# Two conditional MLP layers on one core: a third group of four, another order of units, and the sort of the second layer's choices off VectorE

## The chip, the cores and the metric

The kernel runs on one core of a Trainium2 chip, all in float32. The metric is the device time of one execution in microseconds (us); the number compared is the median of the runs. Engines are named as in the profile: PE (TensorE), DVE (VectorE), ACT (ScalarE), POOL (GpSimd), SP (SyncE, which here issues most DMAs); PEld is PE's weight load.

## The reference

There are 16 batches of 256 rows by 256 features, and 8 numbers for each batch that choose experts. Two layers are added to the input one after the other.

```python
# layer one: one expert of 8 for each batch
expert = jnp.argmax(opcode_onehot, axis=-1)
up   = x @ W_up[expert].T + b_up[expert]        # 256 -> 512
gate = x @ W_gate[expert].T + b_gate[expert]
x = x + (silu(up) * gate) @ W_down[expert].T + b_down[expert]

# layer two: the two best experts of 8, weighted, and one shared expert
w, sel = top_k(softmax(router_logits), 2);  w = w / w.sum()
mlp(x, g, u, d) = (gelu(x @ g) * (x @ u)) @ d   # 256 -> 1024 -> 256
x = x + sum_k w[k] * mlp(x, expert sel[k]) + mlp(x, shared)
```

So layer one has 16 pieces of work (a batch with its expert), layer two has 32 chosen pieces and 16 that all use the shared expert.

## The kernel before

**Units.** Pieces that use the same expert are put together. A `Pair` takes two pieces of one expert and multiplies the two batches by the weights with a seven-product scheme in place of eight (`STEPS`): seven products for each quarter of the hidden width, on sums of weight blocks (`sums_q`, `sums_d`, made by POOL) and sums of the inputs (`sums_b`, on DVE). A first-layer pair has 2 quarters, a second-layer pair 4. A product is two matmuls of 128x128 by 128x256, and the profile has two PE passes for each float32 matmul. ACT copies a bank (L637), DVE combines copies and banks (L645), ACT applies silu or gelu, DVE multiplies by the other half (L708) and makes the sums for the down product. The seven down products of a pair (`down`, L746) are not run at its end: `line.later` puts them between the up products (L660) of the unit that follows, from `first` on and `step` apart. A `Single` does one piece by plain products. A `Quad` takes four batches of the shared expert with 26 products (`BLOCK`) for each of two halves of the hidden width, in place of 28 for two pairs; its weight factors are made once by `prepare`, which POOL and ACT run between the second-layer pairs, and wait in DRAM. `SEEDS`, `SUMS_AT`, `DOWNS_AT`, `ACT_AT` and `ACT_SUMS_AT` say after which product of a group a bank is seeded, sums are made, the downs of the group before run, and activations follow. The banks of PSUM are given out by `bank` in the order they come free.

**Order.** Each engine runs its instructions in the order written. `Line` writes it: `main` advances a clock with each product, `later` queues work for a clock time, `quarter` is called at each quarter and issues loads for the fifth quarter ahead and POOL's sums for the third ahead. The shared expert's first `2 * NF` batches are done by pairs (`shared`), the other by groups of four: `NF = 4` gives four pairs and two groups. The order of units is

1. two first-layer singles, then the first-layer pairs that are certain (four, `l0_pairs`);
2. a branch on a number made on the device (`arms(0)`): how many further pairs layer one has (`l0_more`). The profile's counts show three for this input. In this arm the shared pairs and the further first-layer pairs take turns: shared, further, shared, further, and so on;
3. the second-layer pairs (`pairs`), a second branch (`arms(1)`; three more pairs here), two second-layer singles and the groups of four.

`announces` says at which quarters each engine gets a hint of the arm to come, so that its code can be fetched.

**The choices.** To find what can be paired, the pieces are ordered by expert with comparisons of all with all. For layer one this runs at the start on 128 partitions (16x16 comparisons, same on each partition). For layer two `choices` computes the second-best experts and weights and `order_of_work` sorts the 32 pieces: comparisons of 32x32, so 1024 elements on each of 128 partitions, in twelve large steps and more small ones on DVE. These steps are not run at once: a `Recorder` (L251) stores each as a step, `routes` says how many are run at a quarter, and `route` runs them (so they stand in the profile under one line, L1459). All must be done before the second-layer pairs begin.

Of the kernel before, what the change touches and what calls it, by code (L numbers as in the profile page):

```python
# [8 lines left out]
F32 = mybir.dt.float32  # L9
I32 = mybir.dt.int32  # L10
AF = mybir.ActivationFunctionType
ALU = mybir.AluOpType
# [3 lines left out]
B, S, D, E = 16, 256, 256, 8  # L16
H0, H1 = 512, 1024
P = 128
# [3 lines left out]
NA = 2 * B  # L22
# [1 line left out]
NP1 = (B - 1 - E + 1) // 2  # L24
NP2 = (NA - E) // 2
NS1, NS2 = B - 1 - 2 * NP1, NA - 2 * NP2
NF = 4
N2 = 2 * S
QW = 2 * 4 * P
QB = QW + 4  # L30
# [29 lines left out]


RATIOS = (-1, 0, 1, 2)
BLOCK = ('P0', 'P1', 'P2', 'Q0', 'P3', 'W01', 'Q1', 'Q2', 'W02', 'N01', 'N10', 'Q3', 'W23', 'N02', 'N20', 'W12', 'N32', 'N23', 'W13', 'W03', 'N21', 'N13', 'N12', 'N03', 'N31', 'N30')
SEEDS = {'P1': ('01',), 'P2': ('02',), 'W02': ('23',), 'Q3': ('12',), 'W12': ('03',), 'N10': ('13',)}
SUMS_AT = ((4, (0, 2)), (4, (1, 2)), (10, (2, 3)), (22, (1, 3)), (30, (0, 3)))
DOWNS = (0, 2, 4, 1, 5, 3, 6)
DOWNS_AT = (8, 11, 12, 15, 19, 25, 27, 27, 33, 39, 46, 48, 49, 50)
ACT_AT, ACT_SUMS_AT = 10, 6
QUADS = (B - 2 * NF) // 4
FACTORS = 4  # L70
CHUNKS = 2 * len(BLOCK) // FACTORS
# [3 lines left out]
def kernel(  # L75
# [10 lines left out]
    nc = tc.nc  # L86
    SP, POOL, PE, DVE, ACT = (
        getattr(mybir.EngineType, e) for e in ("SP", "Pool", "PE", "DVE", "Activation")
    )
    ctx.enter_context(tc.manual_schedule())  # L90

    const = ctx.enter_context(tc.tile_pool(name="const", bufs=1))
# [10 lines left out]
    areas = {}  # L103
# [97 lines left out]
    def bank(of, seeded=False, half=False):  # L201
        ok = [i for i in psum["idle"] if psum["filled"][i] or not seeded]
        if psum["halves"]:
            ok = [i for i in ok if (i in psum["halves"]) == half]
            if not seeded and not half:
                ok.sort(key=lambda i: psum["filled"][i])
        assert ok, (of, seeded, psum, open_banks)
        i = ok[0]
        psum["idle"].remove(i)
        assert of not in open_banks  # L210
        open_banks[of] = i
        psum["filled"][i] = not half
        return banks[i]

    def done_with(of):
        psum["idle"].append(open_banks.pop(of))
# [22 lines left out]
    num = const.tile([P, NA], F32, name="num")  # L239
# [6 lines left out]
    ats = const.tile([P, NA], F32, name="ats")  # L246

    made = {}
    steps = [[]]

    class Recorder:  # L251


        def __getattr__(self, name):
            return lambda *args: steps[-1].append(partial(getattr(nc.vector, name), *args))

        @staticmethod
        def step():
            steps.append([])
# [5 lines left out]
    def as_index(v, dst, src, shift, most):  # L265
        v.tensor_scalar(dst, src, float(shift), float(most), ALU.add, ALU.min)
# [113 lines left out]
            v.tensor_scalar(nwsort, wsort, -1.0, None, ALU.mult)  # L380


    exs = [const.tile([P, n], I32, name=f"exs_{i}") for i, n in enumerate((B, NA))]
    bs = [const.tile([P, n], I32, name=f"bs_{i}") for i, n in enumerate((B, NA))]
    wsort = const.tile([P, NA], F32, name="wsort")
    nwsort = const.tile([P, NA], F32, name="nwsort")
    wts = const.tile([P, 2, B], F32, name="wts")
    more = const.tile([P, 1], F32, name="more")
    MOST = ((NS1 - 1) // 2, NS2 // 2)
    more_i = [const.tile([P, 1], I32, name=f"more_{i}") for i in range(2)]  # L390
# [3 lines left out]
    def choices(v):  # L394

        tt, red = v.tensor_tensor, v.tensor_reduce
        hot = [const.tile([P, B, E], F32, name=f"hot_{k}") for k in range(2)]
        tt(hot[0], em8b, over_experts(at1), ALU.is_equal)
        step(v)
        lg2 = const.tile([P, B, E], F32, name="lg2")  # L400
        v.tensor_scalar(lg2, hot[0], -2.0, 1.0, ALU.mult, ALU.add)
        step(v)
        v.scalar_tensor_tensor(lg2, lg2, FLT_MAX, lg, ALU.mult, ALU.min)
        step(v)
        first_largest(v, lg2, 2, at2)
        step(v)
        tt(hot[1], em8b, over_experts(at2), ALU.is_equal)
        step(v)
        v.tensor_scalar(ats, ats, float(-E), -1.0, ALU.max, ALU.min)
        tot = const.tile([P, B], F32, name="tot")  # L410
        red(tot, rw, AX.X, ALU.add)
        step(v)
        v.reciprocal(tot, tot)
        tt(rw, rw, over_experts(tot), ALU.mult)
        step(v)
        for k in range(2):
            tt(hot[k], rw, hot[k], ALU.mult)
            step(v)
            red(wts[:, k, :], hot[k], AX.X, ALU.add)
            step(v)  # L420
        den = const.tile([P, B], F32, name="den")
        tt(den, wts[:, 0, :], wts[:, 1, :], ALU.add)
        v.reciprocal(den, den)
        step(v)
        wsc = const.tile([P, 2, B], F32, name="wsc")
        for k in range(2):
            tt(wts[:, k, :], wts[:, k, :], den, ALU.mult)
        v.tensor_scalar(wsc, wts, SCALE, None, ALU.mult)
        v.scalar_tensor_tensor(wts, wts, 1.0 - SCALE, wsc, ALU.mult, ALU.add)
        step(v)  # L430
        order_of_work(v, NA, ats, 1)


    at_num = const.tile([P, 2, B], F32, name="at_num")
# [24 lines left out]
    class Unit:  # L459
# [4 lines left out]
        def __init__(self, n, layer, at, batches_at=None):  # L464
            self.n, self.layer, self.at, self.batches_at = n, layer, at, batches_at
            self.kp = KPS[layer]
            self.q, self.s, self.x_from = {}, {}, None

            self.d_from = "d" if layer or self.width == 2 else "s" if at < B - 2 else "xt"
            self.acts = []  # L470
# [99 lines left out]
    class Pair(Unit):  # L570
        width, last = 2, False
        behind = quad = None
        crowded = False
        first, step, apart_banks = 18, None, False
# [281 lines left out]
    class Quad(Unit):  # L856
# [4 lines left out]
        width, last, alone = 4, False, False  # L861
# [232 lines left out]
    class Single(Unit):  # L1094
        width = 1
# [177 lines left out]
    l0_pairs = [Pair(next(names), 0, 2 * i) for i in range(NP1)]  # L1273
    l0_more = [Pair(next(names), 0, 2 * NP1 + 2 * i) for i in range(MOST[0])]
    l0_ones = [Single(next(names), 0, 2 * NP1 + i) for i in range(NS1 - 1)]
    shared = [Pair(next(names), 1, None, (2 * i, 2 * i + 1)) for i in range(NF)]
    quads = [Quad(next(names), None, range(i, i + 4)) for i in range(2 * NF, B, 4)]
    first_quad = quads[0]
    first_quad.x_at = None
    pairs = [Pair(next(names), 1, 2 * i) for i in range(NP2)]  # L1280
# [5 lines left out]
    l0_pairs[0].behind = 1  # L1286
    for u in l0_pairs[:-1]:
        u.first = 16.5
    units = [l0_pairs, pairs[:-1]]
    tails = [shared[:1], pairs[-1:]]  # L1290


    announces = [
        [(l0_pairs[0], 0, [SP, POOL, ACT, DVE]), (l0_pairs[2], 1, [PE])],
        [
            (pairs[-7], 0, [SP]),
            (pairs[-5], 0, [POOL, ACT]),
# [5 lines left out]
    among = {  # L1303
        u: [[] for _ in range(u.kp)]
        for u in [*l0_pairs, *l0_more, *pairs, *more_pairs, *shared, *quads]
    }
# [25 lines left out]
    class Line:  # L1332
# [115 lines left out]
        def routes(self, unit, j):  # L1448


            if not unit.layer:
                return {2: 5, 3: 1, 5: 1, 6: 1}.get(self.at, 0)
            return 2 if unit is shared[1] and j < 3 else int(unit is not shared[0] or j > 0)

        def route(self):

# [25 lines left out]
    nc.vector.tensor_scalar(sort1, at1, float(-E), -1.0, ALU.max, ALU.min)  # L1482
    nc.vector.memset(sort1[:, 0:1], 0.0)
    order_of_work(nc.vector, B, sort1, 0, [partial(l0_first.up, j) for j in range(2)])
    choices(Recorder())
    steps.append([partial(give, "ys", "sq")])
    l0_one.load_q(0)
    l0_one.load_x()
# [43 lines left out]
    run(units[0])  # L1532
    for k in arms(0):

        mid, further = [], l0_more[:k]
        for i, u in enumerate(shared[:NF]):
            mid.append(u)
            if i < len(further):
                mid.append(further[i])
                u.step = 4  # L1540
        places = [a for u in mid for a in among[u]]
        for a in places:
            a.clear()
        pieces = [p for u in l0_ones[2 * k :] for p in (u.ups, u.downs)]
        for a, p in zip(places[4:], pieces):
            a.append(p)
        follow([*mid, *units[1], *tails[1]], behind=False)
        run([*mid, *units[1]])
        while line.routed < len(steps):
            line.route()  # L1550
        for k in arms(1):
            assert not line.preparing
            left = ones[2 * k :]
            rest = [*tails[1], *more_pairs[:k], *left[:-1], *quads, *left[-1:]]
            quads[-1].alone = not left
            last_pair = [*tails[1], *more_pairs[:k]][-1]
            last_pair.first, last_pair.step, last_pair.apart_banks = 14, 3, True
            for u in left[-1:]:
                u.x_from = "at"
            turns["xs"], turns["d"] = [0, 1], [*turns["d"], 2]  # L1560
            for u in rest:
                among[u] = [[] for _ in range(u.kp)]
            follow(rest)
            run(rest)
            line.flush(1 << 30)
            line.send()
# [58 lines left out]
```

## Time and profile before

| | |
|---|---|
| median of 3 runs | 1035.84 us (1035.65 to 1036.08) |
| profiled execution | 1034.93 us, of which span 1033.3 us |
| granted PE clock | 0.999 |
| PE | 1025.3 us busy, 4714 passes |
| DVE | 786.9 us busy |
| POOL | 494.3 us busy |
| ACT | 384.0 us busy |
| DMA | 156.97 MB, mean 152 GB/s |
| first-layer pairs in a row | about 24 to 91 us |
| shared and further first-layer pairs in turns | about 91 to 290 us |
| groups of four | from 868 us |

Busy time of PE is from the start of the first to the end of the last of overlapping passes, so a short stop between two passes hardly shows in it; the distance between starts shows it. The windows of the profile count passes, which shows the same.

### The profile page before, as it was taken

The page shows a single profiled execution, that of the slowest core. Times are in us where ns is not written, and L with a number is a line of the kernel's source. Part 1 is how long each engine was busy: PE and PEld are TensorE (multiplying, and loading weights), DVE is VectorE, ACT ScalarE, POOL GpSimd, SP SyncE. Part 2 cuts the span into 40 slices and gives each one's busy share as a digit, 9 for nine tenths or more (in the row PEclk, how much of TensorE's full clock was granted, in tenths as well). Part 3 has the DMA queues.
Part 4 walks back from the last instruction along what each step waited for, and adds up shares of the span by engine and source line. Part 5 has one row for each costly group of instructions (what it writes and reads, how often), then busy time and mean ns, then how long its engine had stood idle before and what let it go on. Part 6 is the DMA issues. An engine that isn't in the chain of part 4 may idle for free.

```text
span 1033.3 us, 14372 instructions
## 1 busy us (share of the span) xinstructions
PE 1025.3 (99%) x4714; PEld 894.5 (87%) x4714; DVE 786.9 (76%) x1250; ACT 384.0 (37%) x613; POOL 494.3 (48%) x553
## 2 busy tenths in 40 slices
PE   9999999999999999999999999999999999999998
PEld 7888888888888888888888888888888888888887
DVE  8899988878687878878777777778777643997661
ACT  2444353535333324333333333333333323653410
POOL 3965341312464889799567557638754301000001
PEclk9999999999999999999999999999999999999999
DMA  7655647466554576566335534514543455553423
GB/s 262 231 184 193 229 166 229 164 194 214 163 184 132 148 189 170 176 175 173 86 98 143 129 94 125 142 58 129 143 122 110 106 170 130 199 183 95 113 49 76
DMA packets 70528, 156.97 MB, mean 152 GB/s; under 512 B 8226, under 2 KB 38818, under 8 KB 66978
## 3 DMA queue, kind: packets, MB, share of 16 engines
q1 hardware_dynamic: 57170, 140.38, 41.0%
q0 software_dynamic: 12976, 15.21, 10.4%
q8 instruction: 43, 0.70, 0.3%
q14 instruction: 51, 0.42, 0.1%
q10 hardware_dynamic: 288, 0.26, 0.1%
HBM read 124.89 MB, written 30.93 MB: 151 GB/s over the span
## 4 chain that ended last, share of the span: by engine, by line
PE 93%; DVE 3%; POOL 2%; issue 1%; ACT 0%; DMA 0%; SPq 0%; POOLq 0%; DVEq 0%; ACTq 0%
PE bank L660 48%; PE bank L746 30%; PE bank L1030 9%; PE bank L1103 4%; PE bank L1136 2%; DVE c L645 1%; DVE bt L708 1%; PE bank L231 1%; POOL s L595 0%; DMA bt<-x_dram 0%; POOL s L597 0%; POOL s L598 0%; DVE bt L588 0%; POOL s L596 0%; ACT c L702 0%
## 5 line engine op out<-in xcount | busy, mean ns | idle before, releaser
L637 ACT ACTIVATE cp<-bank 128x512 f32<-128x512 f32 x270 | 160.9, 596 | 417.4 <-PE bank L660 416.9
L660 PE MATMUL bank<-xt,s 128*128 128x256 f32 x1216 | 288.6, 380 | 1.2 <-DVE c L645 1.2
L660 PEld LDWEIGHTS bank<-xt,s 128*128 128x128 f32 x1216 | 230.1, 190 | 35.4 <-DVE c L645 1.6
L645 DVE TENSOR_TENSOR c<-cp,bank 128x512 f32<-128x512 f32 x360 | 233.9, 679 | 35.1 <-ACT cp L637 17.7
L660 PE MATMUL bank<-xt,q 128*128 128x256 f32 x912 | 219.7, 379 | 0.0
L746 PE MATMUL bank<-bt,ds 128*128 128x256 f32 x816 | 195.7, 379 | 0.3 <-DVE dz L763 0.3
L660 PEld LDWEIGHTS bank<-xt,q 128*128 128x128 f32 x912 | 173.3, 190 | 23.6
L708 DVE TENSOR_TENSOR bt<-c 128x1024 f32<-128x1024 f32 x90 | 129.2, 1436 | 77.6 <-ACT c L702 75.6
L746 PEld LDWEIGHTS bank<-bt,ds 128*128 128x128 f32 x816 | 154.9, 190 | 22.0 <-POOL s L598 0.7
L557 POOL DMA_DIRECT2D out_dram<-ys x46 | 49.6, 1169 | 240.0 <-DVE ys L779 118.7
L746 PE MATMUL bank<-bt,d 128*128 128x256 f32 x572 | 137.0, 379 | 0.0
L746 PEld LDWEIGHTS bank<-bt,d 128*128 128x128 f32 x572 | 108.7, 190 | 14.8
L595 POOL TENSOR_TENSOR s<-q 128x256 f32<-128x256 f32 x78 | 77.8, 998 | 82.7 <-PE bank L660 49.7
L598 POOL TENSOR_TENSOR s<-s,q 128x256 f32<-128x256 f32 x78 | 66.2, 849 | 98.0 <-PE bank L660 91.3
L702 ACT ACTIVATE c<-c 128x1024 f32<-128x1024 f32 x76 | 79.9, 1051 | 9.7 <-DVE c L645 9.7
L588 DVE TENSOR_TENSOR bt<-bt 128x512 f32<-128x512 f32 x105 | 81.9, 780 | 0.5 <-DMA bt<-x_dram 0.5
L596 POOL TENSOR_TENSOR s<-s,q 128x256 f32<-128x256 f32 x78 | 77.5, 994 | 6.1
L597 POOL TENSOR_TENSOR s<-q 128x256 f32<-128x256 f32 x78 | 74.1, 950 | 0.2 <-PE bank L660 0.2
L590 DVE TENSOR_TENSOR bt<-bt 128x256 f32<-128x256 f32 x98 | 62.0, 633 | 3.4
L595 POOL TENSOR_TENSOR ds<-d 128x512 f32<-128x512 f32 (+1 forms) x21 | 24.7, 1178 | 79.1 <-DMA d<-wd_dram 51.0
L589 DVE TENSOR_TENSOR bt<-bt 128x256 f32<-128x256 f32 x98 | 59.3, 605 | 3.4
L1030 PE MATMUL bank<-xt,q 128*128 128x256 f32 x224 | 50.8, 379 | 0.0
(211 smaller groups left out, 1028.4 us busy)
## 6 DMA issues: line engine op xcount, KB each, us to landing
q<-wq_dram SPq DMA_DIRECT2D x98, 512.0 KB, 4.0
d<-wd_dram SPq DMA_DIRECT2D x19, 1024.0 KB, 5.8
q<-factors SPq DMA_DIRECT2D x26, 512.0 KB, 3.2
xt<-x1d SPq DMA_DIRECT2D x46, 256.0 KB, 5.0
out_dram<-ys POOLq DMA_DIRECT2D x46, 256.0 KB, 5.2
s<-qsums SPq DMA_DIRECT2D x12, 512.0 KB, 5.8
ds<-dsums SPq DMA_DIRECT2D x4, 1024.0 KB, 7.4
d<-wd_dram SPq DMA_DIRECT2D x7, 513.0 KB, 6.5
```

What stands on the lines that cost most here:

```text
L588: tt(more[:, 0:2, :], t[:, 0:3:2, :], t[:, 2:4, :], ALU.subtract)
L595: tt(s("S1"), a("A21"), a("A22"), ALU.add)
L596: tt(s("S2"), s("S1"), a("A11"), ALU.subtract)
L597: tt(s("nS3"), a("A21"), a("A11"), ALU.subtract)
L598: tt(s("nS4"), s("S2"), a("A12"), ALU.subtract)
L637: nc.scalar.activation(t, self.banks["X", j], AF.Copy)
L645: nc.vector.tensor_tensor(self.c[j][:, block].rearrange("p m s -> p (m s)"), self.copies[n, j], self.banks[tag, j], op,)
L660: nc.tensor.matmul(self.banks[tag, j][:, bass.ts(m, S)], lhsT=self.q[j][:, m, A_AT[a], :] if a in A_AT else self.s[j][:, m, S_AT[a], :], r ...
L702: nc.scalar.activation(u, u, AF.Gelu_apprx_tanh)
L708: nc.vector.tensor_tensor(t[:, 0:4, :], u, v, ALU.mult)
L746: nc.tensor.matmul(d, lhsT=src[:, j, :], rhs=self.act_block(j, b), start=OPENS[k] and j == 0, stop=j == self.kp - 1, skip_group_check=True,)
L1030: nc.tensor.matmul(dst[:, bass.ts(m, S)], lhsT=w[:, m, :], rhs=rhs, start=fresh and m == 0, stop=True, skip_group_check=True,)
```

## The change

`NF` goes from 4 to 2: two shared pairs and three groups of four. The order of products in a group, its seeds and the times of its sums, downs and activations are set anew. The two branches keep their places in the program's logic, but the first one stands after two first-layer pairs instead of four; in its arm the other two certain pairs and the further ones run in a row, and the shared pairs follow. Single pieces of layer one that are left over (none for this input) are spread over the shared pairs' quarters.

The second layer's sort is written anew (`order_by_expert`). It holds the 32 pieces on 32 partitions, so that a comparison of all with all is 32 elements on each. POOL makes the comparisons, small matmuls with a matrix of ones turn rows into columns and add over partitions, ACT copies each result out of PSUM, DVE does the parity and the conversions to integers. POOL makes three constant tiles at the start (memsets and two affine selects). From the seventh quarter on one step runs at each first-layer quarter.

```diff
-NF = 4
+NF = 2
-BLOCK = (... 'Q3', 'W23', 'N02', 'N20', 'W12', ... 'N12', 'N03', 'N31', 'N30')
-SEEDS = {'P1': ('01',), 'P2': ('02',), 'W02': ('23',), 'Q3': ('12',), 'W12': ('03',), 'N10': ('13',)}
-SUMS_AT = ((4, (0, 2)), (4, (1, 2)), (10, (2, 3)), (22, (1, 3)), (30, (0, 3)))
+BLOCK = (... 'Q3', 'W23', 'N20', 'N02', 'W12', ... 'N12', 'N30', 'N31', 'N03')
+SEEDS = {'P1': ('01',), 'P2': ('02',), 'W02': ('23',), 'W23': ('12',), 'W12': ('03',), 'N10': ('13',)}
+SUMS_AT = ((4, (0, 2)), (8, (1, 2)), (10, (2, 3)), (22, (1, 3)), (30, (0, 3)))
-DOWNS_AT = (8, 11, 12, 15, 19, 25, 27, 27, 33, 39, 46, 48, 49, 50)
-ACT_AT, ACT_SUMS_AT = 10, 6
+DOWNS_AT = (8, 11, 12, 17, 19, 25, 27, 29, 33, 43, 48, 48, 49, 50)
+ACT_AT, ACT_SUMS_AT = 9, 5
...
+    eye, before = piece_of_z(NA), piece_of_z(NA)
+    for t, op in ((eye, ALU.is_equal), (before, ALU.is_gt)):
+        nc.gpsimd.memset(t, 1.0)
+        nc.gpsimd.affine_select(
+            t, t, pattern=[[1, NA]], compare_op=op, fill=0.0, base=0, channel_multiplier=-1
+        )
+    every = piece_of_z(P)
+    nc.gpsimd.memset(every, 1.0)
+    def order_by_expert(v, g):
...
+        def products(dst, *pairs):
+            def f():
+                b = bank("order", half=True)[: pairs[0][0].shape[1]]
+                for i, (lhsT, rhs) in enumerate(pairs):
+                    k = rhs.shape[1]
+                    nc.tensor.matmul(
+                        b[:, i * k : (i + 1) * k], lhsT=lhsT, rhs=rhs,
+                        start=i == 0, stop=True, skip_group_check=True,
+                    )
+                nc.scalar.activation(dst, b[:, : dst.shape[1]], AF.Copy)
+                done_with("order")
+            step(v)
+            steps[-1].append(f)
+            step(v)
+        products(
+            column,
+            (ats[0:1, :], every[0:1, 0:1]),
+            (wts.rearrange("p k b -> p (k b)")[0:1, :], every[0:1, 0:1]),
+            (before, single),
+        )
+        g.tensor_scalar(grid, ats[:n], at, None, ALU.is_equal)
+        g.tensor_tensor(lower, grid, before, ALU.mult)
+        g.tensor_tensor(grid, grid, lower, ALU.subtract)
+        g.tensor_scalar(key, at, float(n), index, ALU.mult, ALU.add)
+        products(counts, (grid, single), (lower, single))
...
+        products(keys, (every[:, :n], cell))
...
+        products(pos, (grid, single))
...
+        products(found, (every, wide))
...
-        order_of_work(v, NA, ats, 1)
+        step(v)
...
-    units = [l0_pairs, pairs[:-1]]
-    tails = [shared[:1], pairs[-1:]]
+    units = [l0_pairs[:2], pairs[:-1]]
+    tails = [l0_pairs[2:], pairs[-1:]]
-        [(l0_pairs[0], 0, [SP, POOL, ACT, DVE]), (l0_pairs[2], 1, [PE])],
+        [(l0_pairs[0], 0, [SP, POOL, ACT, DVE]), (l0_pairs[1], 1, [PE])],
...
-                return {2: 5, 3: 1, 5: 1, 6: 1}.get(self.at, 0)
-            return 2 if unit is shared[1] and j < 3 else int(unit is not shared[0] or j > 0)
+                return {2: 5, 3: 1, 5: 1, 6: 1}.get(self.at, int(self.at > 6))
+            return int(unit is not shared[0] or j > 0)
...
-        mid, further = [], l0_more[:k]
-        for i, u in enumerate(shared[:NF]):
-            mid.append(u)
-            if i < len(further):
-                mid.append(further[i])
-                u.step = 4
+        further, singles = l0_more[:k], l0_ones[2 * k :]
+        mid = [*tails[0], *further, *shared]
+        for u in [*tails[0], *further][:-1]:
+            u.first = 16.5
+        for u in further:
+            u.crowded = True
```

## The prediction

> **What bounds the kernel now.** I read the page first, then the groups by shape, the chain of waits, the windows of some 18 us, and last the timeline around the places where PE loses time. The page and the groups:
>
> ```profile
> PE 1025.3 (99%) x4714; PEld 894.5 (87%) x4714; DVE 786.9 (76%) x1250; ACT 384.0 (37%) x613; POOL 494.3 (48%) x553
> PE 93%; DVE 3%; POOL 2%; issue 1%; ACT 0%; DMA 0%; SPq 0%; POOLq 0%; DVEq 0%; ACTq 0%
> ```
>
> PE is busy 99% and is 93% of the chain, so the number of its passes is the first thing to count. The 379 ns of a pass in the groups overlaps the next one; the real step is in the chain, whose stretches repeat with every second-layer pair:
>
> ```profile
> 440.55 6.04 PE bank L660 x28
> 476.81 6.04 PE bank L660 x28
> ```
>
> 36.26 us for a pair's 168 passes is 0.2158 us each, and 4714 x 0.2158 = 1017.3 us of the 1033.3. The other 16 us are: start and warm-up to 6.9 us (the six wide passes there stand in for 1.3 us, so 5.6), the tail after PE's last pass (4.6), and some 5.6 us of small stops of PE. The windows say where those are:
>
> ```profile
> 60.50:78.60 18.10, 18.10 (x86) 15.93 (x85) 17.45 (x29) 9.18 (x16) 11.57 (x14) 1.00 0.68 232
> 169.00:187.00 18.00, 17.50 (x80) 14.61 (x79) 16.64 (x29) 7.27 (x11) 0.00 (x0) 1.00 0.61 209
> 187.00:205.00 18.00, 18.00 (x85) 15.73 (x85) 15.72 (x22) 10.14 (x17) 7.78 (x9) 1.00 0.49 168
> 295.00:313.00 18.00, 17.54 (x81) 15.18 (x81) 13.84 (x19) 6.49 (x11) 12.60 (x12) 1.00 0.36 112
> ```
>
> Columns: window, length, busy us and count of PE, PEld, DVE, ACT, POOL, clock, DMA, GB/s. A full window has 85 or 86 passes; two have 80 and 81. The first one in the timeline:
>
> ```profile
> 179.40 1.22 DVE L1459 TENSOR_TENSOR ys<-z,num 128x1024 f32<-128x1024 f32 x1
> 180.53 1.22 DVE L708 TENSOR_TENSOR bt<-c 128x1024 f32<-128x1024 f32 x1
> 181.67 1.28 DVE L645 TENSOR_TENSOR c<-cp,bank 128x512 f32<-128x512 f32 x2
> 182.40 1.13 PE L660 MATMUL bank<-xt,s 128*128 128x256 f32 x4 [0.50 <-DVE c L645]
> ```
>
> A sorting step (L1459) and a gate product stand in DVE's queue ahead of the combine that frees a bank, and PE waits. All such stops after 100 us are where a shared pair ends and the next unit's up passes run without down passes between them. By start-to-start distances of PE's passes beyond 0.216 us they cost 0.49 (123 to 130), 1.15 (178 to 185), 0.49 (233 to 240) and 1.16 us (288 to 299): 3.29 in all. From 60 to 115 us, with first-layer pairs in a row, there is none; in the groups of four, from 868 us on, there is none before the tail at 1019.
>
> **The change, part by part.** *Two shared pairs become one group of four.* A second-layer pair has 4 x 7 x 2 + 7 x 4 = 84 matmuls of two passes, so two have 336 passes; a group has 2 x 26 x 2 + 14 x 4 = 160 matmuls, 320 passes. 16 x 0.2158 = -3.45 us, all on the path. The group's other work must hide. In 870 to 937 us, the densest stretch (first group, mostly no downs), DVE is busy 58.1 of 67 us and PE loses nothing; a middle group has its predecessor's downs between its products and so is slower (some 69 us a group), with less DVE per us. Its loads (13 chunks of 512 KB) meet a DMA at 0.57. The new order has one seed a place later (W23 instead of Q3, so two products, 1.7 us, between seed and use instead of three). A DVE seed is 0.69 us. I put the third group and the new order at +0.2 (0 to +2 should seeds come late six times by 0.3).
>
> *Order of choices.* Twelve steps on 128x1024 (1.21 to 1.24 us each) and wsort's second half, 13 in all, 15.9 us with some 3 us of small ones, leave DVE; nine small ones of about 0.18 us come back (1.6 us). PE gets eight matmuls, 16 passes, in five groups (6, 4, 2, 2, 2), ACT five small copies, POOL 16 operations on 32 partitions. Narrow passes are not in the trace. Ends: 0 and the full step, 16 x 0.216 = 3.45 us, which would eat the whole gain above. I take 1.6: the nearest weight-load row is 190 ns for 128 columns and it hides under the pass before; behind a pass of a few columns it does not, so each group lays one of 190 ns open (0.95), and eleven inner passes at a quarter of a step, having 32 of 128 stationary columns, add 0.6. The Trainium skill ("TensorE: Matmul & The Clock Gate", section LDWEIGHTS) has load time follow the columns and not the rows, 32 / 1.2 = 27 ns for the narrow ones; with that the groups would cost 1.2 us and the sum be 0.4 lower.
>
> Waits added: PE waits for POOL ahead of the four later groups, and behind it stands everything. In the built order POOL's operations for a group stand at least one quarter (some 9 us) before it, and only one block of four sums (0.7 to 1.2 us each) can lie between; I take 0, at most 1 us a group. POOL waits for ACT's copy, and the next sums stand behind; those are made three quarters early. POOL's five setup operations come before its memsets of at_num, which DVE reads at 10.10 us; POOL is idle from 2.5 to 5.0 and then to 19.2, so 0.
>
> One rule speaks against more POOL work here. Two rows of one operation show it:
>
> ```profile
> 60.24 0.42 DVE L590 TENSOR_TENSOR bt<-bt 128x256 f32<-128x256 f32 x1
> 67.68 0.83 DVE L590 TENSOR_TENSOR bt<-bt 128x256 f32<-128x256 f32 x1
> ```
>
> The slow one runs beside a POOL sum. Sixteen narrow POOL operations at 0.2 us (as DVE's small ones) could take at most 1.6 us from DVE over five quarters; DVE has 0.65 us free in each 18.1 us, and no longer has the 1.2 us steps. So 0. The skill ("GPSIMD Engine Reference", Key points) states such contention for operations with two SBUF inputs; it gives no price, and the sum by it is the same.
>
> *First-layer pairs in a row.* Now shared, first-layer, shared, first-layer and so on give four such ends; after, there is one (first shared into second), as the list of PE's products in the built order shows: one run of 36 up products without a down after the start, where there were four. Second-layer pairs among themselves have had none at 0.2 us except 0.44 at 390 us, which stays. 3.29 becomes 0.49 to 1.16; I leave 0.8 and take -2.5 (ends -2.8 and 0). The cover for five more first-layer stretches is DVE at 17.45 of 18.1 us, without sorting steps, as in the 60.5 window. Six ACT table loads (1.28 us) go too; ACT has half its time free, so 0.
>
> *Early stretch.* At 58.6 us PE stops 0.5 us for a DVE dz that stands behind a gap-free DVE queue since 42 us, in which the removed 1.24 us step at 45.5 lay. -0.3 (0 to -0.5). The stop at 43.5 us lies before it and stays.
>
> Sum: -3.45 + 0.2 + 1.6 - 2.5 - 0.3 = -4.45 us. The profiled execution took 1034.93 us (span 1033.3 and 1.6 around it), so 1030.5; the median of the runs is 0.9 above it, so **1031.4**. By the kind ends, -3.45 - 2.8 - 0.5 = -6.75 us: 1029.1.
>
> **Rivals.** *The narrow products cost as much as wide ones and PE restarts after each.* The restart after a stop shows as 354 and 291 ns, 0.21 over two steps. 16 x 0.216 + 5 x 0.21 = 4.5 us, and if half of the stops stay (-1.2), -3.45 - 1.2 + 4.5 = -0.15: 1035.7, no change. For it: nothing of this width was seen. Against: every 190 ns weight load here fits into a step of 216.
>
> *DVE becomes the bound in the first-layer row (slower).* A pair has three sets of sums (L588, L589, L590): 1.5 us a set alone, 2.9 beside POOL. In the 60.5 window they took 6.8 us; all slow, 8.6. Then DVE needs 17.45 + 1.8 = 19.3 us of 18.1: +1.15 us for each of five pairs, 5.7, and the time is 1031.4 + 5.7 = 1037.1. It decides from an excess of 0.9 us a pair. Against: POOL was busy 10 to 12 us of 18 there already.
>
> *Code arrives late at the first branch.* PE's hint for it is now 25.0 us ahead (63.6 and 88.6 us); after, 40 passes, 8.6 us. A GpSimd branch whose code was not there took 2.8 us to its next instruction (78.1 to 80.9), while PE's sequencer ran 2.7 us ahead of its passes: 0 to 2.8 us, 1034.2.
>
> **How the numbers follow.** What this kernel's measurement can tell from no change is about 0.2%, 2.1 us: faster means below 1033.8. Forecast 64%, narrow products 16%, DVE 10%, late code 10%. Half of the late-code and some of the narrow-product cases stay below 1033.8: faster 0.70, same 0.17, slower 0.13 (DVE, and the worst of the products). The range, 1029.2 to 1035.2, leaves out DVE's case and half of the first rival's.
>
> **What would show it.** Right: 4698 wide passes and 16 narrow ones; starts of the passes around a narrow group 0.2 to 0.5 us later than the count of wide passes gives; one stop of 0.5 to 1.2 us at the end of the first shared pair; no 128x1024 sorting steps on DVE; the third group without stops. Wrong: a narrow group that costs 1 us or more, windows of the first-layer row with under 84 passes and PE waiting for DVE L645, or stops in the groups of four waiting for seeds.

## The result, and the profile after

The changed kernel takes 1039.56 us (median of 7, 1036.92 to 1042.31) against 1035.65 us before on the same chip (7 runs, 1034.96 to 1037.05): ratio 1.0036, 95% interval 1.0021 to 1.0051. It is slower, where 1031.4 us was forecast. The profiled execution took 1042.31 us, its span is 1040.7, 7.4 more than before.

The page of the changed kernel (busy time and number of instructions by engine; then the chain that ended last):

```profile
span 1040.7 us, 14363 instructions
PE 1024.2 (98%) x4714; PEld 893.6 (86%) x4714; DVE 782.1 (75%) x1250; ACT 383.8 (37%) x624; POOL 498.2 (48%) x574
PE 93%; DVE 2%; POOL 2%; issue 1%; DMA 1%; ACT 0%; SPq 0%; POOLq 0%; ACTq 0%
```

PE is still what bounds it, and still issues 4714 passes, of which 16 are now the narrow ones (L426). Second-layer pairs run exactly as before, 36.26 us from one repetition in the chain to the next:

```profile
410.38 6.04 PE bank L758 x28
446.64 6.04 PE bank L758 x28
```

So the loss lies in single places. The windows (window, length, busy us and count of PE, PEld, DVE, ACT, POOL, granted clock, DMA share, GB/s) show them:

```profile
54.00:58.60 4.60, 1.64 (x8) 1.13 (x7) 4.53 (x6) 1.29 (x3) 4.52 (x6) 1.00 0.38 121
58.60:63.00 4.40, 4.40 (x13) 3.55 (x14) 2.92 (x6) 1.82 (x3) 1.06 (x1) 0.61 0.02 6
66.00:84.00 18.00, 18.00 (x84) 15.79 (x84) 15.64 (x26) 8.71 (x15) 10.68 (x16) 1.00 0.54 176
162.00:180.00 18.00, 17.44 (x81) 15.05 (x81) 17.30 (x29) 6.75 (x9) 5.86 (x5) 1.00 0.87 313
184.00:202.00 18.00, 17.56 (x80) 14.57 (x79) 15.17 (x22) 7.43 (x12) 7.98 (x10) 1.00 0.75 260
1032.40:1040.60 8.20, 0.00 (x0) 0.00 (x0) 0.42 (x1) 0.00 (x0) 0.00 (x0) 0.71 0.14 31
```

First row: eight passes in 4.6 us. Second row: thirteen where twenty fit, because the granted clock was 0.61. Third row: the first-layer pairs in a row run without a stop, with VectorE at 15.6 of 18 us. Fourth and fifth: the two unit ends that still lose passes. Last row: 8.2 us after PE's last pass in which only one VectorE operation runs (before, 4.6 us from last pass to end). The first two rows in the timeline, and the wait that the profile gives for them:

```profile
54.61 1.03 PE L844 MATMUL bank<-bt,ds 128*128 128x256 f32 x4
58.57 0.73 PEld L758 LDWEIGHTS bank<-bt,q 128*128 128x128 f32 x4 [3.34 <-issue]
58.60 1.12 PE L758 MATMUL bank<-bt,q 128*128 128x256 f32 x4 [2.96 <-issue]
59.54 1.89 PE L844 MATMUL bank<-bt,ds 128*128 128x256 f32 x4
```

"Issue" means that no semaphore explains the wait. The trace's records of branches do: PE's sequencer (the part that takes the instructions in order and runs ahead of the passes) reaches the first branch at 54.28 us, and that branch instruction takes 3.98 us (before: at 88.61 us, 0.44 us). During it a 16 KB packet moves on queue q8 of the page (55.72 us), which is taken to be PE's code: its packets follow PE's progress through the program. The four passes at 59.54 last 1.89 us instead of 1.03; starts are some 427 ns apart where 216 is the step, eight times, and then it is over; the record of the granted clock has 0.5 from 59.55 us on, for 3.41 us.

At the other end SyncE makes two branches to leave the arm. They lie 0.49 us apart before (1027.81, 1028.30) and 3.90 us apart after (1031.88, 1035.78), and what follows takes the same time in both.

### The profile page after: what moved, and what is told of

It reads as the page before. It is cut to its first block, busy times and chain, and to the rows that moved or that the text cites. A ratio compares the mean times of both kernels' runs of the same rounds, so it can differ in the third digit from the quotient of the medians.

```text
span 1040.7 us, 14363 instructions
## 1 busy us (share of the span) xinstructions
PE 1024.2 (98%) x4714; PEld 893.6 (86%) x4714; DVE 782.1 (75%) x1250; ACT 383.8 (37%) x624; POOL 498.2 (48%) x574
## 4 chain that ended last, share of the span: by engine, by line
PE 93%; DVE 2%; POOL 2%; issue 1%; DMA 1%; ACT 0%; SPq 0%; POOLq 0%; ACTq 0%
PE bank L758 44%; PE bank L844 30%; PE bank L1128 13%; PE bank L1201 4%; PE bank L1234 2%; DVE c L743 1%; DVE bt L806 1%; DMA q<-wq_dram 0%; POOL s L693 0%; POOL s L695 0%; POOL s L696 0%; POOL s L694 0%; ACT c L800 0%; POOL out_dram L655 0%; DVE bt L686 0%
## 5 line engine op out<-in xcount | busy, mean ns | idle before, releaser
L735 ACT ACTIVATE cp<-bank 128x512 f32<-128x512 f32 x246 | 146.6, 596 | 386.3 <-PE bank L758 386.1
L758 PE MATMUL bank<-xt,s 128*128 128x256 f32 x1088 | 257.6, 379 | 0.7 <-DVE c L743 0.7
L743 DVE TENSOR_TENSOR c<-cp,bank 128x512 f32<-128x512 f32 x328 | 211.9, 678 | 30.4 <-ACT cp L735 17.6
L758 PEld LDWEIGHTS bank<-xt,s 128*128 128x128 f32 x1088 | 206.3, 190 | 30.1 <-DVE c L743 1.1
L806 DVE TENSOR_TENSOR bt<-c 128x1024 f32<-128x1024 f32 x82 | 118.8, 1449 | 78.3 <-ACT c L800 77.8
L758 PEld LDWEIGHTS bank<-xt,q 128*128 128x128 f32 x816 | 155.0, 190 | 21.1
L693 POOL TENSOR_TENSOR s<-q 128x256 f32<-128x256 f32 x78 | 76.7, 983 | 91.0 <-PE bank L758 63.8
L696 POOL TENSOR_TENSOR s<-s,q 128x256 f32<-128x256 f32 x78 | 68.7, 881 | 86.2 <-PE bank L758 86.2
L694 POOL TENSOR_TENSOR s<-s,q 128x256 f32<-128x256 f32 x78 | 78.2, 1003 | 6.1
L800 ACT ACTIVATE c<-c 128x1024 f32<-128x1024 f32 x68 | 71.5, 1051 | 9.3 <-DVE c L743 9.3
L1128 PEld LDWEIGHTS bank<-xt,q 128*128 128x128 f32 x336 | 63.7, 190 | 9.4 <-DVE ds L1153 0.6
L1128 PE MATMUL bank<-s,q 128*128 128x256 f32 x288 | 66.4, 379 | 0.0
L688 DVE TENSOR_TENSOR bt<-bt 128x256 f32<-128x256 f32 x94 | 62.3, 663 | 3.2
```

Of the source, the lines that this page charges most:

```text
L693: tt(s("S1"), a("A21"), a("A22"), ALU.add)
L694: tt(s("S2"), s("S1"), a("A11"), ALU.subtract)
L696: tt(s("nS4"), s("S2"), a("A12"), ALU.subtract)
L735: nc.scalar.activation(t, self.banks["X", j], AF.Copy)
L743: nc.vector.tensor_tensor(self.c[j][:, block].rearrange("p m s -> p (m s)"), self.copies[n, j], self.banks[tag, j], op,)
L758: nc.tensor.matmul(self.banks[tag, j][:, bass.ts(m, S)], lhsT=self.q[j][:, m, A_AT[a], :] if a in A_AT else self.s[j][:, m, S_AT[a], :], r ...
```

## Where the 7.4 us of the profiled executions are

By distances between starts of passes beyond 0.216 us, after minus before:

| | us |
|---|---|
| 16 wide passes fewer | -3.45 |
| 16 narrow passes and getting in and out of them | +2.18 |
| stops at unit ends after 100 us (3.29 to 1.88) | -1.41 |
| stop at the start of the third group of four, near 920 us | +0.52 |
| wait at 1022.6 us ahead of the last products (0.17 to 0.75) | +0.58 |
| stop at the first branch, 3.13 and 0.08 after it, and eight slow steps | +4.87 |
| stops at 43.5 and 58.6 us | -0.35 |
| start, a load waited for at 7.9 us | +0.77 |
| from the last pass to the end (4.6 to 8.3) | +3.70 |
| sum | +7.4 |

The start varies from run to run (0 to 0.8 us over the profiled executions below). Two rows turn the gain into a loss: the first branch and the end.

## Experiments

Theory: the program's code arrives late in two places, at the first branch, which the change moved from 88 to 54 us, and at SyncE's last branches; everything else saves time. Rivals: the hint's short lead alone does it; the new program is late wherever the branch stands; the narrow products or VectorE eat the gain.

**The same again, three hints, and an arm fewer.** *again* is the changed kernel unchanged.

> The changed kernel once more, unchanged, for a second profile and more times. Theory (code): the 3.3 us stop of PE at the first branch (54 to 58 us), the eight slow steps behind it and SP's 3.9 us at the end of the program belong to the program and come back within 0.5 us each; the 1.4 us wait for weights at 8 us and what else differs is chance. Rival (chance): one of the three is absent here, and the spread of 1036.9 to 1042.3 us of the first runs is made of them.

Measured: 1039.63 us, ratio 1.0032 (1.0020 to 1.0043). The branch took 3.24 us, PE stopped 2.45 us, and seven steps were slow: the stop is there again, though 0.7 us shorter. SyncE's two branches at the end lie 3.60 us apart.

*hint_first* gives PE's hint together with those of the other engines, *no_hint* gives none:

```diff
-        [(l0_pairs[0], 0, [SP, POOL, ACT, DVE]), (l0_pairs[1], 1, [PE])],
+        [(l0_pairs[0], 0, [SP, POOL, ACT, DVE, PE])],    # hint_first
+        [(l0_pairs[0], 0, [SP, POOL, ACT, DVE])],        # no_hint
```

> PE's hint for the first branch is given with the other engines' at the first quarter of the first pair, some 20 us earlier; nothing else changes. Theory (PE's code for the arm is not there yet because its hint, 8.7 us ahead, came after the last fetch of code before the branch): the stop at the branch falls from 3.3 us to under 0.5, the slow steps (427 ns) go with it, and the time falls by about 4.9 us, to some 1034.7. Rival (the hint does nothing here, the branch is always a miss in this place): the same stop and the same time as the changed kernel.

> PE gets no hint for the first branch; nothing else changes. Theory (the late hint is as good as none): the same stop of 3.3 us and the same 427 ns steps behind it. Rival (the late hint brought the code part of the way): a stop of 4 us or more.

Measured: hint_first 1039.33 us, ratio 1.0038 (1.0024 to 1.0052); no_hint 1042.89 us in its one run. With the hint 31.6 us ahead of the branch instead of 8.7, PE still stops 2.80 us. Without a hint it stops 3.97 us. The lead, by which the prediction measured this risk, is not what counts; the hint saves only some 1 us here, by one execution without it.

*arms_four* cuts the second branch to four arms, so that this input's arm is the last (an input that needs a fifth is not served):

```diff
-    MOST = ((NS1 - 1) // 2, NS2 // 2)
+    MOST = ((NS1 - 1) // 2, NS2 // 2 - 1)
```

> The second branch has four arms (none to three further pairs) instead of five, so this input's arm is the last one and the jump at its end is short; the work done for this input is the same. Theory (SP's 3.9 us at the end is the fetch of the code behind the fifth arm, too far for what was fetched ahead): that step falls to 0.5 us as in the kernel before, the time between PE's last pass and the end from 8.3 to about 4.7 us, the whole time by 3.5 us. Rival (the 3.9 us are chance, or come from the end of the program whatever lies between): no change.

Measured: 1036.47 us, ratio 1.0007 (0.9998 to 1.0016). SyncE's two branches are 0.49 us apart again, the last pass to the end takes 5.1 us. The stop at the first branch is unchanged (2.66 us).

**The branch back at its old place.** *branch_four* puts all four common pairs ahead of the first branch and the hint where it was; its arms with fewer than two further pairs are not kept right, and this input takes none of them (nor, in mid_arms, the arm with none). *late_arms* is the same with four arms in the second branch; *mid_arms* has three pairs ahead and the four arms; *before_four* is the kernel before with four arms.

```diff
-    units = [l0_pairs[:2], pairs[:-1]]
-    tails = [l0_pairs[2:], pairs[-1:]]
+    units = [l0_pairs[:4], pairs[:-1]]                        # mid_arms: l0_pairs[:3]
+    tails = [[*l0_pairs[4:], *l0_more[:2]], pairs[-1:]]       # [*l0_pairs[3:], *l0_more[:1]]
-        [(l0_pairs[0], 0, [SP, POOL, ACT, DVE]), (l0_pairs[1], 1, [PE])],
+        [(l0_pairs[0], 0, [SP, POOL, ACT, DVE]), (l0_pairs[2], 1, [PE])],   # l0_pairs[2], 0
...
-        further, singles = l0_more[:k], l0_ones[2 * k :]
+        further, singles = l0_more[2:k], l0_ones[2 * max(k, 2) :]   # 1 in place of 2
...
```

> The changed kernel, but with the first branch after all four common first-layer pairs (near 90 us, as before the change) and TensorE's hint where it was before; the arms that this input does not take are not kept right. Theory A, the code is late only because the branch now stands near 54 us: no stop at the branch and no slow steps of 427 ns after it, so 2.5 to 5 us less of TensorE's time than in the changed kernel, whose stop took 2.4 to 3.1 us and was followed by 0 to 1.7 us of slow steps: 1035.4 us (1034.0 to 1036.5), with SyncE's end still 8 us after the last pass. Rival B, the code of this program is late wherever the branch stands: 1039.5 us, the stop at 90 us instead.

> The same with the second branch cut to four arms, so that the arm of this input is the last and no engine jumps over a fifth one at the end. Theory A: 1035.4 less the 3.1 us that four arms saved in the changed kernel, 1032.3 us (1031.0 to 1033.5), faster than before the change; it is what the prediction's sum gave with both stops of late code away. Rival B: 1036.5 us.

> As the one with four arms in the second branch, but the first branch one pair later than in the changed kernel (near 72 us) and TensorE's hint 26 us ahead of it. If what matters is that TensorE fetches at least one block of code in order between the hint and the branch (it does so near 57 to 60 us): 1032.3 us, no stop. If the branch must stand as far from the start as it did before: a stop of 2.5 to 4 us near 73 us and 1036.5 us.

> The kernel before, with only the second branch cut to four arms. Theory C, SyncE's jump over the fifth arm was nearly free there (0.49 us, the last pass to the end 4.6 us) and turned dear only in the changed kernel: 1035.4 us (1034.6 to 1036.2). Rival D, the jump costs some 3 us in both programs and the difference of the tails came from elsewhere: 1032.5 us.

Measured: branch_four 1032.45 us, ratio 0.9968 (0.9957 to 0.9980); late_arms 1032.95, 0.9975 (0.9966 to 0.9984); mid_arms 1034.03, 0.9986 (0.9976 to 0.9995); before_four 1036.78, 1.0010 (1.0001 to 1.0020).

Moving this branch, with PE's hint for it, gives 7.1 us and makes the changed kernel faster than before. The stop and the slow steps are gone (the branch takes 0.34 us), and the end was shorter as well, 5.5 us, which had not been expected: SyncE's two branches at the end lie 0.50 us apart, with all five arms in place. So the jump over the fifth arm has no fixed price, four arms bring nothing more in late_arms, and rival D is out: in the kernel before, the jump takes 0.49 us with four arms as with five. The 3.1 us of arms_four belong to the changed kernel's arrangement. Why SyncE's code is late at the end in one program and not in another is not shown. The kernel before with four arms was 0.6 us above the range of theory C, with an end of 6.1 us: there SyncE went on 4.8 us after its last branch instead of 3.3, so the other waits of the end vary too. The page of branch_four, and its windows at the old stop and in the first-layer row:

```profile
span 1032.2 us, 14360 instructions
PE 1023.3 (99%) x4714; PEld 892.7 (86%) x4714; DVE 781.9 (76%) x1250; ACT 384.0 (37%) x624; POOL 497.6 (48%) x574
```

```profile
54.00:72.00 18.00, 17.84 (x87) 15.19 (x86) 16.89 (x28) 8.41 (x15) 10.95 (x17) 1.00 0.54 170
60.50:78.60 18.10, 18.10 (x86) 15.87 (x84) 16.98 (x29) 9.02 (x16) 10.72 (x16) 1.00 0.56 176
```

mid_arms had PE's code in time, yet was 1.1 us slower than late_arms: VectorE's own branch, at 77.80 us, came late there (3.65 us to its next instruction), and PE stopped 1.8 us for VectorE from 81 to 84 us. Code can be late on each engine by itself.

**Why the place is bad.** In branch_four, late_arms and mid_arms PE fetches its next 16 KB at 54.1 to 54.6 us, which is where the changed kernel branches. *shift_16* and *shift_6* add 16 or 6 narrow products near 25 us whose results nobody uses; they move that fetch ahead of the branch and cost 1.3 and 0.7 us by the trace. *shift_16_no* also drops PE's hint.

```diff
     l0_one.ups()
+    b = bank("order", half=True)
+    for i in range(16):                                  # 6 in shift_6
+        nc.tensor.matmul(b[:NA, i : i + 1], lhsT=before, rhs=every[:NA, 0:1], ...)
```

> The changed kernel with 16 more narrow products ahead of the first-layer pairs, near 25 us, whose results nobody uses: 64 more instructions for TensorE before the first branch, so that it comes to its next 16 KB of code 32 wide passes or 6.9 us earlier against the branch, still after its hint. They cost 1.2 us. Theory E, the hint acts at that fetch: no stop at the branch, 2.4 to 4.8 us saved, 1036.3 us (1034.8 to 1038.3), and a fetch some 7 us ahead of the branch in the trace. Rival F: the stop stays, 1040.8 us.

> The same with 6 more narrow products: 24 instructions, 2.6 us, at a cost of 0.6 us. Theory E: the fetch starts 2.5 to 3.5 us ahead of the branch and the stop shrinks to under 1 us: 1036.5 us (1035 to 1038). Rival F: 1040.2 us.

> 16 more narrow products and no hint for TensorE at the first branch. Theory E: the fetch 7 us ahead brings the code that follows in order, and the branch stops TensorE for some 4 us as in the changed kernel without a hint (4.2 us): 1041 to 1044 us. If the extra products help whatever the hint does: no stop, 1036.3 us.

Measured: 1038.98 us, ratio 1.0035 (1.0021 to 1.0049); 1038.58, 1.0033 (1.0021 to 1.0044); 1039.63, 1.0040 (1.0025 to 1.0056). From the traces, all in us:

| kernel | PE's hint | PE's code fetches before the branch | branch reached | it took | stop of PE | slow steps |
|---|---|---|---|---|---|---|
| before | 63.6 | 60.2, 83.7 | 88.6 | 0.44 | 0 | 0 |
| changed | 45.6 | 29.4 | 54.3 | 3.98 | 3.13 | 8 |
| hint_first | 21.4 | 31.5 | 53.0 | 3.65 | 2.80 | 0 |
| no_hint | none | 32.3 | 54.1 | 4.73 | 3.97 | 12 |
| branch_four | 63.6 | 54.1, 77.8 | 89.5 | 0.34 | 0 | 0 |
| mid_arms | 53.8 | 54.5, 59.9 | 71.5 | 0.34 | 0 | 0 |
| shift_6 | 45.4 | 24.2, 49.5 | 54.1 | 0.45 | 0 | 0 |
| shift_16 | 46.7 | 24.0, 49.7 | 55.6 | 0.34 | 0 | 0 |
| shift_16_no | none | 23.0, 50.1 | 54.8 | 3.63 | 2.81 | 0 |

Theory E holds for PE in the traces, one profiled execution each: with the hint some 9 us ahead as in the changed kernel, the branch stops nothing once a fetch starts 4.6 us or more ahead of it, and without the hint the same fetch, at the same time, is of no use. That the hint changes what the fetch brings is inferred from this. It does not cover hint_first, where a fetch follows the hint too, at 31.5 us, 21.5 us ahead of the branch, and PE still stops; why stays open.

The times do not show it: all three lie outside their expected ranges, shift_16 and shift_6 above, shift_16_no below, and shift_16_no with its stop is only 0.65 us above shift_16 without one. The times of shift_16 and shift_6 fell by only 0.6 and 1.0 us, not by 3, and the trace of shift_16 says why. VectorE's branch is late in the changed kernel too (2.85 us), hidden behind PE's own stop. With PE in time it shows:

```profile
65.86 1.28 DVE L743 TENSOR_TENSOR c<-cp,bank 128x512 f32<-128x512 f32 x2 [2.85 <-PE bank L758]
66.60 1.13 PE L758 MATMUL bank<-bt,q 128*128 128x256 f32 x4 [1.03 <-DVE c L743]
68.41 0.89 PE L844 MATMUL bank<-bt,ds 128*128 128x256 f32 x3 [0.67 <-DVE ys L877]
```

VectorE reached its branch at 62.82 and went on at 65.70; its idle time, which the profile puts down to PE, is that. PE loses 2.2 us to it from 65.2 to 68.7, the stop near 60.8 us is back (0.5), and the added products cost 1.3: 4.0 us, against the 2.9 to 4.9 that PE's branch had cost.

**The parts of the change, on top of branch_four (1032.45 us).**

```diff
-                for i, (lhsT, rhs) in enumerate(pairs):            # narrow_twice
+                for i, (lhsT, rhs) in [*enumerate(pairs)] * 2:
-    order_by_expert(Recorder(nc.vector), Recorder(nc.gpsimd))      # old_sort
+    order_of_work(Recorder(nc.vector), NA, ats, 1)
-NF = 2                                                             # nf4
+NF = 4
```

*old_block* takes BLOCK, SEEDS, SUMS_AT, DOWNS_AT and the two ACT constants from the kernel before.

> The changed kernel with its first branch after four pairs (1032.45 us), and every narrow product of the choices issued twice. Reading of the trace: a group costs its inner steps of 31 to 53 ns, one or two of 95 to 200, and 0.2 us for getting out of and back into the wide passes (309 and 320 ns for 216), 2.18 us for the five; the second copies add inner steps alone, some 0.7 us: 1033.1 us. First rival of the prediction, each narrow product is as dear as a wide pass: 3.5 us more, 1035.9 us.

> The changed kernel with its first branch after four pairs, but layer two's choices ordered as before the change, by VectorE on 128x1024 tiles, one step a quarter; no narrow products. Theory A, those steps of 1.2 us stop TensorE in the first-layer row, where VectorE is busy 17.5 of 18.1 us: 2.2 us saved, stops of 0.5 to 1 us in each of five pairs added, 1032.8 to 1035.3 us. Rival B, VectorE has room for them and the new ordering only costs: 1030.3 us.

> The changed kernel with its first branch after four pairs, but with four shared pairs and two groups of four, as before the change. Prediction's term: 16 passes of 0.2158 us more, 3.45, less the 0.5 us that TensorE stops at the first group in the changed kernel: 1035.4 us (1035 to 1036). Rival, the third group gives its gain back by stops or slower VectorE: 1032.5 to 1033.5 us.

> The changed kernel with its first branch after four pairs, with the old order of products, seeds, sums and down products in the groups of four. Prediction's term, the new order is worth 0 to 2 us either way and was put at 0.2 together with the third group: 1032.2 us (1031.9 to 1033.0), and the stop of 0.5 us at the first group near 915 us gone if the new order made it. Rival, the new order is what lets three groups follow one another without stops: 1034 us or more.

Measured: narrow_twice 1033.30 us, ratio 0.9976 (0.9966 to 0.9987); old_sort 1037.49, 1.0016 (1.0007 to 1.0025); nf4 1035.92, 1.0002 (0.9992 to 1.0011); old_block 1032.87, 0.9970 (0.9958 to 0.9982).

Doubling the narrow products adds 0.85 us, 0.67 of it in the groups themselves by the trace: they are not as dear as wide passes. The first group in the changed kernel's timeline:

```profile
65.64 0.22 PE L426 MATMUL bank<-z,ats 1*32 1x1 f32 x2
65.72 0.20 PE L426 MATMUL bank<-z,wts 1*32 1x1 f32 x2
65.79 0.20 PE L426 MATMUL bank<-z 32*32 32x1 f32 x2
65.91 0.92 PE L758 MATMUL bank<-bt,s 128*128 128x256 f32 x3
```

Six passes start within 0.27 us; the wide pass before takes a step of 309 ns and the first one after 320.

The new ordering is the part that pays in this row. With the old one, PE stops ten times from 56 to 139 us, 7.6 us in all. The waits of old_sort there (engine and work waited for: us, times, longest), a full window, and one such stop in the timeline:

```profile
PEld bank L758 <- DVE c L743: 4.7, 5, 1.4
PE bank L758 <- DVE c L743: 2.8, 3, 1.0
```

```profile
96.00:114.00 18.00, 16.17 (x73) 13.31 (x73) 17.43 (x33) 7.88 (x13) 12.01 (x14) 1.00 0.48 157
```

```profile
103.97 1.22 DVE L1557 TENSOR_TENSOR z<-key 128x1024 f32<-128x1024 f32 x1
105.44 1.28 DVE L743 TENSOR_TENSOR c<-cp,bank 128x512 f32<-128x512 f32 x2
106.18 1.13 PE L758 MATMUL bank<-bt,s 128*128 128x256 f32 x4 [0.80 <-DVE c L743]
```

73 passes where 84 fit, VectorE at 17.4 of 18 us: it has no room for steps of 1.2 us among first-layer pairs. Going back to it costs 5.0 us, more than the 0.3 to 2.8 expected.

nf4 costs 3.5 us, as much as its 16 passes. Neither of its groups starts with the stop of 0.52 us that branch_four has near 915 us, at the start of its third group, while old_block has that stop at the same size: it comes with the third group, not with the new order, whose worth is 0.4 us by the medians, within their spread. The 3.5 us are a net, and that they equal the passes is partly chance: nf4 has another stop, 1.7 us at 992 us, and lacks two stops of branch_four, 0.8 us near 165 and 1.0 us from 180 to 191, where its first shared pair ends.

At this end both kernels run the same products without downs between them. The first four lines are branch_four's, the last two nf4's:

```profile
180.81 1.01 DVE L688 TENSOR_TENSOR xt<-xt 128x256 f32<-128x256 f32 x1
180.81 0.72 POOL L693 TENSOR_TENSOR s<-q 128x256 f32<-128x256 f32 x1 [14.76 <-PE bank L758]
181.74 1.75 DVE L806 TENSOR_TENSOR bt<-c 128x1024 f32<-128x1024 f32 x1
191.04 1.13 PE L758 MATMUL bank<-xt,s 128*128 128x256 f32 x4 [0.43 <-DVE c L743]
179.75 0.42 DVE L688 TENSOR_TENSOR xt<-xt 128x256 f32<-128x256 f32 x1
180.47 1.22 DVE L806 TENSOR_TENSOR bt<-c 128x1024 f32<-128x1024 f32 x1 [0.29 <-ACT c L800]
```

With two shared pairs, GpSimd makes weight sums (L693 to L696) at this end, VectorE's operations beside them take 1.01 and 1.75 us, and PE stops; with four, GpSimd is idle from 176 to 193 us, the same operations take 0.42 and 1.22 us, and PE does not stop. So the end of a unit alone need not cost anything. No run moves these sums alone, and none puts the old order of units back alone.

## Why the prediction was wrong

**What failed.** The step "Code arrives late at the first branch": priced at 0 to 2.8 us, given 10%, and argued by the hint's lead. The central sum put it at nothing. Measured, the stop is 2.4 to 3.1 us in four profiled executions with a hint, and up to 1.7 us of slow steps follow, which the prediction did not price: 2.9 to 4.9. Two rows of before were carried to the new place and did not hold there. The branch took 3.2 to 4.0 us instead of GpSimd's 2.8, and PE's sequencer came to the branch 1.05 to 1.2 us before the step of the last pass ahead of it ended, where at the old place that was 2.7 us: less of the branch was hidden. And it is not the hint's lead that decides but the place of the branch against PE's fetches. The rows for that were in the trace of before: fetches of 16 KB at 31.2, 60.2 and 83.7 us, the last one 4.9 us ahead of the branch that cost nothing. The second failed step is unspoken: the sum took the 4.6 us after the last pass as fixed. They became 8.3, and were 4.6 to 8.5 in the kernels run here.

**What held.** The groups' term: 3.45 forecast, 3.5 measured as a net of several stops (above); the 16 passes fewer are counted. The first-layer row does not make VectorE the bound: no stop there with the new ordering. The narrow products are far from wide passes: 2.18 us against 1.6 (the 1.2 that the prediction gave by the page's load time is further off). The five open loads, forecast at 0.95, are the two edges of each group (309 and 320 ns for 216: 0.98); the passes inside cost 1.2 instead of 0.6, because the last of each group takes 95 to 200 ns.

**What was off in size.** Stops at unit ends went from 3.29 to 1.88, not 0.8. One has a step of the new ordering in it. The changed kernel near 170 us:

```profile
169.28 1.29 DVE L1557 TENSOR_SCALAR exs<-z 128x32 int32<-128x32 f32 x1
170.57 0.47 DVE L861 SCALAR_TENSOR_TENSOR dz<-bank,d,bt 128x256 f32<-128x256 f32 x1
171.19 1.10 PE L844 MATMUL bank<-bt,ds 128*128 128x256 f32 x4 [0.56 <-DVE dz L861]
```

The conversion of the sorted experts takes 1.29 us beside a GpSimd sum (the next one, which meets a sum for 0.04 us only, 0.17) and stands ahead of the dz that PE needs (0.80 us lost). It takes as long in late_arms, mid_arms, nf4 and shift_6, where PE loses nothing there; in late_arms VectorE comes to it some 1 us earlier against PE's products. Another, 0.7 us near 195, is the end of the first shared pair as forecast, with GpSimd's sums beside it. The third group was put at 0.2 and stops PE 0.52, and the wait ahead of the last products (+0.58) was not in the sum.

With both late places out of the way (branch_four) the kernel takes 1032.45 us, 1.05 above the forecast and inside its range; its gain is 3.1 us where 4.45 were summed. The profiled execution of branch_four was the slowest of its six (1033.78 us), so the terms are read from the places and the sum from the medians.

## What to carry to other kernels

When an edit moves a branch, look in the trace for the engine's code fetches on both sides of its new place, on every engine; a hint helped here only where a fetch followed it 4.6 to 16.4 us ahead of the branch, not where the last one was 21.5 us ahead. The end of a kernel is a place of that kind too: count it as an uncertain term, not as a constant. And a stop can cover another engine's: price each engine's late code alone before the gain of mending one is forecast.

## What the runs showed of the hardware

At the two switches, a branch of PE whose code was late took 1.8 to 4.7 us, 0.3 to 0.45 where it was not; packets of code were of 16 KB on q8 (PE) and mostly of 8 KB on q14 (the other engines). At the second switch PE's branch took 2.2 to 2.4 us in *again*, hint_first and no_hint, 0.42 in the first profile of the same program as *again*, and PE's passes did not stop in any of them.

After a stop of some 3 us PE's steps were at times 427 ns instead of 216, and the record of the granted clock has 0.5 for 3.41 us (6.83 after the longest stop): eight after 3.13 us, seven after 2.45, eight after 2.66, twelve after 3.97, none after 2.80 and 2.81. The Trainium skill ("TensorE: Matmul & The Clock Gate", Part 1) says that the clock halves after an idle window of some 3.4 us, and that the window runs freely, so that the same kernel can differ between runs. The second half agrees with the mixed outcomes here; the first does not, since a stop of 2.45 us was enough once. The slow steps (0 to 1.7 us) and the start (0 to 0.8 us) can make up some 2.5 us of the changed kernel's spread of 5.4 us, against 2.1 before; what made the rest is not shown.
